# Unread products, an earlier first block and other ties in a planned instruction order of a four-layer sequence kernel

## The chip, the cores and the metric

The kernel runs on one core of a Trainium2 chip. A core has five engines with a queue each, run in order: TensorE (PE, matrix products; PEld is its weight load), VectorE (DVE), ScalarE (ACT), GpSimd (POOL) and SyncE (SP, which here only issues transfers). The time is device microseconds of one launch. The runs of the kernel before took 2665.15 us in the median of three (2664.05 to 2667.85).

## The reference, cut to what matters

The input is a batch of 32 elements of 256x256 numbers in float32. Each element passes through four layers one after the other; no element depends on another.

```python
def reference(x, ...):                      # x: (32, 256, 256)
    # layer 0: block norm over the whole 256x256, scale and shift made from a time step
    out = silu(scale * layer_norm(x) + shift) @ W_in + b_in
    x = silu(scale * layer_norm(out) + shift) @ W_out + b_out + x
    # layer 1: attention with 16 heads of 16, a bias of 16x256x256 per element and a mask, FF 1024
    x = ln(x) * (1 + scale1) + shift1
    scores = q @ k / 4 + attention_bias     # masked to -inf
    x = x + softmax(scores) @ v @ Wo + bo
    x = x + gelu_sigmoid((ln(x) * g2 + beta2) @ W1 + b1) @ W2 + b2
    # layer 2: finite differences of x times fixed grids, one step in time, max(., 0)
    x = maximum(x + df * dt, 0)
    # layer 3: causal attention with 16 heads, FF 1024, a gate between its input and output
    return x + gate * (block(x) - x)
```

Scale and shift of layers 0 and 1 come from two small networks on sine and cosine encodings of one number per element. They are made once for all 32 elements, ahead of the first element.

## The kernel before, in words

**Tiles.** An element is a tile of 128 partitions x 2 x 256. A full product has a 128x128 stationary operand and streams 256 columns into a PSUM bank; a transpose is a product with the identity that streams 128. In float32 each plain product stands in the trace as two records, a transpose as one. Two kinds of product use small tiles of PE's array: the scores (`scores`, line 834; 32 rows by 128 columns, groups of 8 products that run side by side) and the weighted values (`values`, line 885; 128 rows by 32 columns, groups of 16). All eight PSUM banks are one pool with the tag `bank`; a PSUM tile is named `mm`, `sc` (scores) or `tr` (transposed probabilities).

**Layers.** `layer_0` (line 990), `layer_1` (1015) and `layers_23` (1071) are generators, one per element. `layer_0` makes `offset` on POOL from `beta_t` and the shift, the block statistics in `block_stats` (759; two products with one column each against `mean_mat`), and in `scaled_silu` (780) the row scale `rs` on POOL, `y` on DVE, a Tanh on ACT and a last step on DVE, whose result `th` goes into the products with `l0_win` and, after a second pass, `l0_wout`. `layer_1` reads 16 heads of bias through the tile `nb` (three buffers), subtracts the mask on POOL, adds the bias to the scores on DVE, takes the exponential on ACT (`pr`), transposes it on PE (`turned`, 868) and multiplies by the values. `layers_23` computes the finite differences with the products against `stencil`, then the causal attention and the feed-forward whose hidden tile `hid` is put through Gelu in one ACT instruction (`gelu_all`).

**Setup** (lines 542 to 650): encodings on DVE with Sin on ACT; `conditioning` (606) is a group of small products with `l0w1`, `l0w2`, `l0wss` or `w_ada` streamed, a copy to `by_batch`, a transpose and an add. The three calls in a row for layer 0 make `mod0`, then halved; the fourth makes `mod1`. `gamma_t` and `beta_t` are transposed copies of the tiles `l0gb`. `load_x` (536) loads an element; the first one is loaded ahead of the layers. `turned_vectors` (521) brings in bias vectors as rows (`as_rows`), by 14 small transfers for the second block of them, and transposes them into `cols`. The other weights are loaded by `load_attention`, `load_rest` and `loads`; `load_rest` has a product of `wo` with a bias vector (`L1wo<-cols` and `L3wo<-cols` in the profile), so that PE waits for these two weights to land.

**What sets the order.** No engine call goes out when it is written. `Order` (line 65) records each one with a length, its dependencies and a rank, the time `order.now` at which it is due. `trace` (1155) sets the rank: a layer of element b starts at `b * PERIOD + START[i] + EDGE[b, i]`, each `yield` moves it on by its step times `PACE[i]`, and `SHIFT` corrects single steps. `arrange` (217) then plans: it plays the five engines forward and, whenever one is free, lets it take the ready unit of the lowest rank. A unit is one instruction or, under `together`, a group of products. Its constants stand for the hardware: `HOPS` is the time from an instruction's end to a dependent one on another engine, to which `SLACK` is added when the dependent one is on PE, `CAPS` limits the PSUM tiles of each name, `EARLIER` makes PE's ranks earlier by name, `STAY` and `FRESH` add to a unit's rank on PE if it changes the shape of the array:

```python
                    if e == "pe" and units[u][2][0]["length"][1] != shape:
                        rank += self.STAY
                        if units[u][2][0]["length"][1] != (P, P):
                            rank -= self.PAIR if shape != (P, P) else 0.0
                        elif units[u][2][0]["length"][3] == 2:
                            rank += self.FRESH
```

So `FRESH` falls on a full product (two records) that would follow a small-tile group, and not on a transpose. `emit` (377) issues all calls in the planned order; every instruction stands on the line 382 in the profile (383 after the change). An engine then runs its instructions strictly in that order and waits where an operand or a bank is not ready.

Of the kernel before, what the change touches and what calls it, by code (L numbers as in the profile page):

```python
# [16 lines left out]
AF = mybir.ActivationFunctionType  # L17
# [4 lines left out]
P = 128  # L22
# [16 lines left out]

PERIOD = 86.0
START = (-61.8, 0.0, 116.9)
PACE = (1.55, 1.23, 1.08)
EDGE = {(0, 0): 14.4, (0, 1): -5.0, (0, 2): 5.8, (1, 0): -19.0, (1, 1): -3.8, (1, 2): -0.2, (2, 0): -27.1, (2, 1): -2.0, (2, 2): -1.1, (3, 0): 12.3, (3, 1): 0.4, (3, 2): 0.3, (4, 0): 5.2, (4, 1): 2.3, (4, 2): 0.6, (27, 0): -1.1, (27, 1): -1.0, (27, 2): 0.5, (28, 0): 1.7, (28, 1): -0.3, (28, 2): -2.0, (29, 0): 2.1, (29, 1): -0.1, (29, 2): -2.1, (30, 0): -11.1, (30, 1): 5.7, (30, 2): -4.5, (31, 0): -16.9, (31, 1): 1.9, (31, 2): 15.4}
SHIFT = (
    {0: -93.0, 1: -33.6, 2: -27.5, 3: -32.8, 4: -14.7, 5: -56.4, 6: -42.3, 7: -28.3, 8: 23.1},
    {0: -9.7, 1: -80.2, 2: -10.3, 3: -1.7, 4: 2.7, 5: 8.8, 7: -7.0, 8: 14.7, 9: -90.2, 11: 7.3,
     12: 21.2, 13: -0.4, 14: 4.0, 15: -1.3, 16: 11.4, 17: 5.1, 19: 4.8, 20: 10.4, 21: 46.1, 22: 16.4,
     23: -8.7, 24: -13.1, 25: -30.4, 26: -2.4, 27: -90.0, 28: 8.3, 29: -134.0, 30: -0.4, 31: -13.2,  # L50
     32: -34.6, 33: 0.8, 34: -0.3, 35: 7.7, 36: -2.9, 37: -8.0},
    {0: -1.1, 1: -32.9, 2: -9.3, 3: 27.2, 4: 23.9, 5: -25.6, 6: -48.6, 7: -36.4, 8: -12.9, 9: 6.6,
     11: 3.0, 12: 15.4, 13: -32.5, 15: -6.5, 16: 20.0, 17: -2.0, 18: 6.6, 19: -0.5, 20: 0.4, 21: -82.2,
     23: 9.0, 24: 7.5, 25: 0.1, 26: -11.0, 27: -38.3, 28: 12.2, 29: 7.0, 30: 30.4, 31: 3.6, 32: -8.7,
     33: -46.1, 34: 4.4, 35: 2.3, 36: -58.5, 37: -16.3, 38: -59.7, 39: 18.0, 40: -15.2, 41: 12.6},
    {0: -24.5, 1: -13.3, 2: 6.7, 3: -84.2, 4: 42.8},
)
NORM = 8.0
LAND = 3.0
SQUARE = 2.0  # L60
# [4 lines left out]
class Order:  # L65
# [11 lines left out]
    TURN = 92.0  # L77
    FIRST = {(32, P): 107.0, (P, 32): 27.0, (P, P): 107.0}
    APART = 120.0
    SLACK = 50.0  # L80
    SEEN = {(32, P): 165.0, (P, 32): -16.0, (P, P): 165.0}
    CAPS = {"sc": 8, "tr": 7, "mm": 7}
    EARLIER = {"sc": 29.6, "mm": -2.0, "tr": 6.2}
    STAY = 5.0
    FRESH = 1.0
    PAIR = 0.0
    PORT = 0.05
    TABLES = {AF.Sin: 0, AF.Tanh: 1, AF.Exp: 1, AF.Gelu: 2}
# [342 lines left out]
def kernel(ctx: ExitStack, tc: tile.TileContext, io, out, n_batch=B):  # L431
    nc = tc.nc
    order = Order()
    pe, dve, act, pool, sync = (
        order.engine(name, eng)
        for name, eng in (
            ("pe", nc.tensor), ("dve", nc.vector), ("act", nc.scalar), ("pool", nc.gpsimd), ("sync", nc.sync)
        )
    )
# [8 lines left out]
    ident = ctile("ident", [P, P])  # L448
# [28 lines left out]
    mod0 = ctile("mod0", [P, 2 * C2, B])  # L477
# [19 lines left out]
    def mm_tile(shape):  # L497
        return psum_tile(shape, "mm")
# [37 lines left out]
    def load_x(b):  # L536
        x = sb.tile([P, C2, D], F32, tag="x", name="x")
        sync.dma_start(x, rows(io["x"][b]))
        return x
# [9 lines left out]
    )  # L549
    w1 = sb.tile([P, 4 * E], F32, tag="t2", name="l0w1", bufs=3)  # L550
    sync.dma_start(w1, io["L0_cond_W1"])
    i_b = sb.tile([P, B], I32, tag="nq1", name="i_b")
    sync.dma_start(i_b, io["itok_B_34_63"].partition_broadcast(P))
    w2 = sb.tile([P, 4, 4 * E], F32, tag="hid", name="l0w2", bufs=1)
# [1 line left out]
    wss = sb.tile([P, 2, 4, D], F32, tag="pt", name="l0wss", bufs=3)  # L556
    sync.dma_start(wss[:, 0], rows(io["L0_cond_Wsc"]))
    sync.dma_start(wss[:, 1], rows(io["L0_cond_Wsh"]))
    first_x = load_x(0)
    gb = []  # L560
    for n in ("gamma", "beta"):
        t = sb.tile([P, C2, D], F32, tag="l2", name="l0gb", bufs=4)
# [16 lines left out]
    def cosine(dst, a, r, parts=slice(0, P)):  # L579

        dve.tensor_scalar(a, r, -1.0, None, ALU.mult)
        dve.tensor_tensor(a, a, r, ALU.max)
        dve.tensor_scalar(a, a, -1.0, math.pi / 2, ALU.mult, ALU.add)
        act.activation(dst[parts], a[parts], AF.Sin)

    small = sb.tile([P, 16, B], F32, tag="pr", name="encodings", bufs=10)
    x0, r0, n0, a0, enc, x1f, r1, n1, a1, emb0, emb1 = (small[:, i] for i in range(11))
# [8 lines left out]
    reduced(r1, n1, x1f)  # L596
    act.activation(emb0, r1, AF.Sin)
    cosine(emb1, a1, r1)

    def silu(dst, zh, th, z):  # L600

        dve.tensor_scalar(zh, z, 0.5, None, ALU.mult)
        act.activation(th, zh, AF.Tanh)
        dve.scalar_tensor_tensor(dst, th, 1.0, zh, ALU.add, ALU.mult)

    def conditioning(dst, weights, src, bias):


        pm = mm_tile([P, P])
        with order.together():  # L610
            for k in range(len(weights(0))):
                for j in range(4):
                    pe.matmul(
                        pm[j * B : (j + 1) * B, :], lhsT=src[:, k, :], rhs=weights(j)[k],
                        start=k == 0, stop=k == len(weights(0)) - 1,
                    )
        by_batch = sb.tile([P, P], F32, tag="h_t", name="by_batch")
        dve.tensor_copy(by_batch, pm)
        pm = mm_tile([P, 4, B])
        pe.transpose(pm.rearrange("p j b -> p (j b)"), by_batch, ident)  # L620
        dve.tensor_tensor(dst, pm, bias.unsqueeze(2).broadcast_to([P, 4, B]), ALU.add)
# [6 lines left out]
    part = lambda j: slice(j * P, (j + 1) * P)  # L628
    conditioning(h1, lambda j: [w1[:, part(j)]], enc.unsqueeze(1), vector["L0_cond_b1"])
    silu(h1s, zh, th, h1)  # L630
    conditioning(h2, lambda j: [w2[:, k, part(j)] for k in range(4)], h1s, vector["L0_cond_b2"])
    both = cols0[:, 8:12]
    conditioning(mod0, lambda j: [wss[:, j // 2, k, part(j % 2)] for k in range(4)], h2, both)
# [7 lines left out]
    for i, e in enumerate((emb0, emb1)):  # L641
# [9 lines left out]
    sync.dma_start(parity, io["c_parity"])  # L651
    order.now = START[0] + 5.0
    _, more = turned_vectors(
        "cols1",
        (
            "L1_cond_bq", "L1_cond_bk", "L1_cond_bv", "L1_cond_b1", "L1_cond_g2", "L1_cond_beta2",
            "L3_cond_bq", "L3_cond_bk", "L3_cond_bv", "L3_cond_b1", "L3_cond_gamma1", "L3_cond_beta1", "L3_cond_gamma2", "L3_cond_beta2",
        ), sync,
    )
# [3 lines left out]
    def col(name):  # L663
        return vector[name]
# [33 lines left out]
    def loads():  # L698

        load_rest(l1, "L1", "g2", "beta2")  # L700
        yield LAND

        edge = sb.tile([P, 3, 2, 4], F32, tag="pr", name="edge", bufs=10)
        sync.dma_start(edge, io["c_edge"].rearrange("p (k e x) -> p k e x", k=3, e=2))
        a1 = sb.tile([P, C2, D], F32, tag="l2", name="a1", bufs=4)
        sync.dma_start(g_a0, rows(io["L2_cond_A_grid"][0]))
        sync.dma_start(a1, rows(io["L2_cond_A_grid"][1]))
        sync.dma_start(g_b0, rows(io["L2_cond_B_grid"][0]))
        sync.dma_start(g_b1, rows(io["L2_cond_B_grid"][1]))
        sync.dma_start(g_b2, rows(io["L2_cond_B_grid"][2]))  # L710
        later.stencil = ctile("stencil", [P, 2, C2, NEAR])
        sync.dma_start(later.stencil, io["c_stencil"])
        later.dt_b = load_row("dt_b", io["condB_dt"])
        yield 3 * LAND
        dve.tensor_scalar(g_b0, g_b0, 0.5, None, ALU.mult)
        dve.tensor_scalar(g_b2, g_b2, 0.5, None, ALU.mult)
        dve.tensor_tensor(g_cp, g_b1, a1, ALU.subtract)
        dve.tensor_scalar(g_cp, g_cp, 0.5, None, ALU.mult)
        dve.tensor_tensor(g_cm, g_b1, a1, ALU.add)
        dve.tensor_scalar(g_cm, g_cm, 0.5, None, ALU.mult)  # L720
        e_t = sb.tile([P, C2, 2, 4], F32, tag="small", name="small")
        for c in range(C2):
            dve.tensor_tensor(e_g[:, c], edges4(g_b2)[:, c], edge[:, 0], ALU.mult)
            dve.tensor_tensor(e_t[:, c], edges4(a1)[:, c], edge[:, 1], ALU.mult)
            dve.tensor_tensor(e_dd[:, c], edges4(g_b1)[:, c], edge[:, 2], ALU.mult)
        dve.tensor_tensor(e_dd, e_dd, e_t, ALU.add)
        yield 3 * LAND
        later.l3 = load_attention("L3")
        sync.dma_start(causal, io["c_causal"])
        later.l3_g1, later.l3_beta1 = col("L3_cond_gamma1"), col("L3_cond_beta1")  # L730
        yield 3 * LAND
        load_rest(later.l3, "L3", "gamma2", "beta2")
        later.gate_b = load_row("gate_b", io["condB_gatescore"])
# [421 lines left out]
    def trace(n, gen, layer, start, pace):  # L1155
        i = 0
        while True:
            order.now = start + SHIFT[layer].get(i, 0.0)
            step = next(gen, None)
            if step is None:  # L1160
                break
            start += step * pace
            i += 1

    trace(3 * n_batch, loads(), 3, START[1] + 25.0, 1.0)
    res = {}
    for b in range(n_batch):
        for i, layer in enumerate((layer_0, layer_1, layers_23)):
            trace(3 * b + i, layer(b, res), i, b * PERIOD + START[i] + EDGE.get((b, i), 0.0), PACE[i])
    with tc.manual_schedule():  # L1170
        order.emit()
# [33 lines left out]
```

## Time and profile before

| what | value |
|---|---|
| median of three runs | 2665.15 us |
| the profiled execution | 2665.54 us |
| its span, first to last instruction | 2663.7 us |
| PE, DVE, ACT, POOL busy | 2600.2, 2122.1, 1920.1, 1565.0 us |
| mean granted clock of PE | 0.989 |
| PE's first product starts | 5.52 us |
| last product of the run ends, store follows | 2658.2 us |
| longest waits of PE up to 132 us | 5.5 (first rows of vectors), 3.3 and 3.4 (`th`), 2.8 (encodings), 2.6 (`t`), 2.5 (`x`) |
| longest waits of PE from 2585 us | 4.2 and 3.7 (`hid`), 3.7 (`t`) |

Busy time is the union of an engine's records, so waits and idle time are the rest. The granted clock is what the throttle let PE have: 1.00 or 0.50 at each moment, averaged over a stretch. The timeline merges equal instructions in a row: start, length from the first start to the last end, engine, line, operation, tiles, shape, count, and in brackets the idle time before and what ended it. Ends of products are modelled; starts are not, so prices below are taken from start to start. In the tables of stretches the columns are the stretch, its length, the busy time (and number of records) of PE, PEld, DVE, ACT and POOL, the granted clock, the DMA engines' share and GB/s.

### The profile page before, as it was taken

What the parts mean: (1) busy time and instruction counts of PE and PEld (TensorE: products, weight loads), DVE (VectorE), ACT (ScalarE), POOL (GpSimd) and SP (SyncE); (2) the same over time, 40 slices, a digit from 0 to 9 for tenths busy, and PEclk for the clock granted to TensorE, in tenths of its full rate; (3) what the DMA queues carried; (4) which work ended last, traced back from release to release, by engine and by line L of the source; (5) the groups of instructions that cost most, each with busy time, mean ns of one, the idle gap of its engine ahead of it and who ended that gap; (6) DMA issues with size and microseconds to landing.
All of it is one profiled execution on the core that took longest, in us unless ns stands there. A gap on an engine that the chain in (4) does not pass through costs nothing.

```text
span 2663.7 us, 60400 instructions
## 1 busy us (share of the span) xinstructions
PE 2600.2 (98%) x20462; PEld 2118.4 (80%) x20462; DVE 2122.1 (80%) x7627; ACT 1920.1 (72%) x6120; POOL 1565.0 (59%) x1960
## 2 busy tenths in 40 slices
PE   5999999999999999999999999999999999999997
PEld 4777888888888888888888888888888888888775
DVE  5887888878878877878878878877878887887853
ACT  2677777877777877777777777877777877777854
POOL 3865676555676555576555677555576555676420
PEclk7999999999999999999999999999999999999998
DMA  7321122212122212122212122212122211122100
GB/s 243 110 60 59 42 73 69 70 49 66 45 70 70 70 49 66 46 70 69 70 49 65 43 73 70 69 49 66 46 69 69 70 57 57 42 69 64 45 5 9
DMA packets 177064, 169.69 MB, mean 64 GB/s; under 512 B 19514, under 2 KB 175220, under 8 KB 176756
## 3 DMA queue, kind: packets, MB, share of 16 engines
q1 hardware_dynamic: 176720, 165.82, 20.2%
q8 instruction: 163, 2.67, 0.4%
q14 instruction: 145, 1.19, 0.1%
q10 hardware_dynamic: 36, 0.01, 0.0%
HBM read 157.40 MB, written 8.39 MB: 62 GB/s over the span
## 4 chain that ended last, share of the span: by engine, by line
PE 91%; DVE 3%; ACT 2%; DMA 1%; POOL 1%; issue 1%; SPq 0%; ACTq 0%; POOLq 0%; DVEq 0%
PE mm L382 68%; PE tr L382 14%; PE sc L382 9%; DVE pr L382 1%; ACT hid L382 1%; ACT pr L382 1%; DMA x<-in_x_dram 1%; POOL nb L382 0%; DMA nb<-in_fside_Bx16xSxS_dram 0%; DVE pt L382 0%; ACT L382 0%; POOL rstd L382 0%; DVE gd L382 0%; DMA L1wo<-in_L_cond_Wo_dram 0%; DVE st L382 0%
## 5 line engine op out<-in xcount | busy, mean ns | idle before, releaser
L382 ACT ACTIVATE pr<-pr,mn 128x256 f32<-128x256 f32 (+1 forms) x2048 | 966.9, 478 | 93.0 <-DVE mn L382 91.8
L382 POOL TENSOR_TENSOR nb<-mask_f,nb 128x512 f32<-128x512 f32 x512 | 693.3, 1378 | 114.7 <-DMA nb<-in_fside_Bx16xSxS_dram 101.9
L382 PE MATMUL tr<-ident,pr 128*128 128x128 f32 x3584 | 508.5, 276 | 5.4 <-ACT pr L382 1.8
L382 PEld LDWEIGHTS tr<-ident,pr 128*128 128x128 f32 x3584 | 419.5, 143 | 85.8 <-ACT pr L382 29.1
L382 DVE CUSTOM_DVE_ANT_0 pr<-sc,nb 128x256 f32<-128x256 f32 x1024 | 388.0, 414 | 25.3 <-POOL nb L382 14.0
L382 ACT ACTIVATION_READ_ACCUMULATOR pr<-pr,mn 128x1 f32 x2048 | 398.0, 194 | 0.0
L382 DVE COPY pt<-tr 128x512 f32<-128x512 f32 (+1 forms) x512 | 311.3, 615 | 72.9 <-PE tr L382 72.3
L382 POOL TENSOR_SCALAR hid<-hid 128x256 f32<-128x256 f32 x256 | 100.0, 405 | 433.4 <-ACT hid L382 433.1
L382 DVE CUSTOM_DVE_ANT_0 pr<-sc,causal 128x128 f32<-128x128 f32 (+1 forms) x1024 | 299.3, 352 | 38.5 <-PE sc L382 37.2
L382 PE MATMUL sc<-k_t,nq 32*128 32x256 f32 (+1 forms) x4096 | 269.5, 375 | 0.1
L382 ACT COPY pt<-tr 128x512 f32<-128x512 f32 (+1 forms) x512 | 261.4, 526 | 10.9 <-PE tr L382 6.0
L382 PE MATMUL mm<-L3w,hid 128*128 128x256 f32 x1024 | 241.5, 385 | 10.1 <-ACT hid L382 10.0
L382 PE MATMUL mm<-h_t,L3w 128*128 128x256 f32 x1024 | 247.6, 382 | 1.5 <-DVE h_t L382 1.4
L382 PE MATMUL mm<-h_t,L1w 128*128 128x256 f32 x1024 | 248.9, 381 | 0.0
L382 PE MATMUL mm<-L1w,hid 128*128 128x256 f32 x1024 | 239.0, 380 | 0.1
L382 PEld LDWEIGHTS sc<-k_t,nq 32*128 32x128 f32 x4096 | 163.3, 185 | 73.0 <-issue 25.7
L382 PEld LDWEIGHTS mm<-L3w,hid 128*128 128x128 f32 x1024 | 190.6, 193 | 35.1 <-ACT hid L382 11.9
L382 POOL COPY wide<-rs 128x256 f32<-128x256 f32 x128 | 53.3, 416 | 281.3 <-DVE rs L382 131.8
L382 PEld LDWEIGHTS mm<-L1w,hid 128*128 128x128 f32 x1024 | 186.6, 190 | 23.3 <-issue 1.2
L382 PEld LDWEIGHTS mm<-h_t,L3w 128*128 128x128 f32 x1024 | 184.2, 191 | 22.9 <-DVE h_t L382 2.5
L382 PEld LDWEIGHTS mm<-h_t,L1w 128*128 128x128 f32 x1024 | 183.7, 190 | 23.3 <-issue 1.8
L382 ACT ACTIVATE t<-x,shift,rstd 128x256 f32<-128x256 f32 x128 | 67.2, 590 | 148.8 <-DVE shift L382 148.8
(173 smaller groups left out, 4997.7 us busy)
## 6 DMA issues: line engine op xcount, KB each, us to landing
nb<-in_fside_Bx16xSxS_dram SPq DMA_DIRECT2D x512, 256.0 KB
x<-in_x_dram SPq DMA_DIRECT2D x32, 256.0 KB
out_dram<-d SPq DMA_DIRECT2D x32, 256.0 KB
mask<-in_mask_Bx1xSxS_bk_dram SPq DMA_DIRECT2D x32, 64.0 KB
L1w<-in_L_cond_W_dram SPq DMA_DIRECT2D x2, 1024.0 KB
L3w<-in_L_cond_W_dram SPq DMA_DIRECT2D x2, 1024.0 KB
l0w<-in_L_cond_W_dram SPq DMA_DIRECT2D x1, 1024.0 KB
g_b<-in_L_cond_B_grid_dram SPq DMA_DIRECT2D x3, 256.0 KB
```

Source lines behind the costliest of these rows:

```text
L382: call(*args, **kwargs)
```

## The change

There are four parts.

1. The constants of the planner: `PERIOD`, `START`, `PACE`, `EDGE`, `SHIFT`, and in `Order` `SLACK` from 50 to 0, `CAPS` of `sc` from 8 to 7 and of `tr` from 7 to 5, `EARLIER`, and `FRESH` from 1 to 16.
2. The first element's `x` is loaded right behind `l0w1`, layer 0 of that element is due far earlier (`EDGE[0, 0]` is -796), and what follows the first `silu` of the setup is due at -960 instead of -1000.
3. An ACT instruction of one column with Tanh behind the last cosine.
4. `fill` records products of 64 columns that nobody reads, with a rank so late (1e6) that PE takes one in the plan only where nothing else is ready: 150 that read `mod0`, and 100 that read the last element's output of layer 1.

```diff
-PERIOD = 86.0
-START = (-61.8, 0.0, 116.9)
-PACE = (1.55, 1.23, 1.08)
-EDGE = {(0, 0): 14.4, (0, 1): -5.0, (0, 2): 5.8, (1, 0): -19.0, ...}
+PERIOD = 85.9
+START = (-61.2, 0.0, 116.1)
+PACE = (1.45, 1.23, 1.08)
+EDGE = {(0, 0): -796.0, (0, 1): -5.1, (0, 2): -0.1, (1, 0): -50.0, ...}
...
+FILL = (150, 100)
...
-    SLACK = 50.0
+    SLACK = 0.0
-    CAPS = {"sc": 8, "tr": 7, "mm": 7}
-    EARLIER = {"sc": 29.6, "mm": -2.0, "tr": 6.2}
+    CAPS = {"sc": 7, "tr": 5, "mm": 7}
+    EARLIER = {"sc": 26.8, "mm": -3.3, "tr": 5.8}
-    FRESH = 1.0
+    FRESH = 16.0
...
     sync.dma_start(w1, io["L0_cond_W1"])
+    first_x = load_x(0)
...
-    first_x = load_x(0)
...
     cosine(emb1, a1, r1)
+    act.activation(a1[:, 0:1], emb1[:, 0:1], AF.Tanh)
...
     silu(h1s, zh, th, h1)
+    order.now = -960.0
...
+    def fill(count, src):
+
+        order.now = 1e6
+        for _ in range(count):
+            pe.matmul(mm_tile([P, P // 2]), lhsT=src, rhs=ident[:, 0 : P // 2], start=True, stop=True)
+
+    fill(FILL[0], mod0.rearrange("p j b -> p (j b)"))
     trace(3 * n_batch, loads(), 3, START[1] + 25.0, 1.0)
...
         for i, layer in enumerate((layer_0, layer_1, layers_23)):
+            if (b, i) == (n_batch - 1, 2):
+                fill(FILL[1], res[1, b][:, 0, 0:P])
```

`SHIFT` changes in nearly all its entries, by a few us in most and by up to 110 in single ones.

## Prediction

> **What bounds the kernel now.** I read the page first, then busy time by stretches, then TensorE's own sequence in the first 60 and the last 80 us.
>
> ```profile
> span 2663.7 us, 60400 instructions
> PE 2600.2 (98%) x20462; PEld 2118.4 (80%) x20462; DVE 2122.1 (80%) x7627; ACT 1920.1 (72%) x6120; POOL 1565.0 (59%) x1960
> PEclk7999999999999999999999999999999999999998
> PE 91%; DVE 3%; ACT 2%; DMA 1%; POOL 1%; issue 1%; SPq 0%; ACTq 0%; POOLq 0%; DVEq 0%
> ```
>
> TensorE (PE) is the bound and carries 91% of the chain that ended last. By stretches (columns: length, then PE, PEld, DVE, ACT, POOL busy, granted clock, DMA):
>
> ```profile
> 23.90:132.10 108.20, 88.16 (x573) 66.93 (x573) 78.02 (x263) 56.22 (x176) 71.00 (x87) 0.84 0.55 171
> 300.00:2400.00 2100.00, 2097.78 (x16695) 1720.12 (x16694) 1727.27 (x6207) 1573.06 (x5017) 1283.79 (x1603) 1.00 0.20 61
> 2585.80:2663.70 77.90, 57.53 (x317) 42.15 (x316) 27.45 (x107) 33.01 (x97) 6.66 (x11) 0.85 0.02 7
> ```
>
> In the middle PE waits 2 us in 2100: there only PE's own work counts. At both ends it waits, and runs at a reduced clock (0.84 and 0.85). I priced PE's whole sequence by the median start-to-start of each pair of neighbours in the middle: 2548.7 us of work at full clock, of which 4.5 lie before 24 us, 76.2 before the first stencil product (132.1 us) and 40.8 behind 2585.8. The other 115.0 us of the span are waits and half clock: 56.0 before 132.1, 6.8 from there to 300, 10.1 in the middle, 5.0 from 2400, 37.1 at the end (5.5 of it the last DVE steps and the store).
>
> **Part 1, ties behind small tiles (FRESH 1 to 16, SLACK 50 to 0, CAPS, the retuned times).** All 12606 old products stay, in another order. PE's timeline gives the price of a change of shape:
>
> ```profile
> 2541.46 0.94 PE L382 MATMUL sc<-k_t,nq 32*128 32x128 f32 x16
> 2542.32 1.13 PE L382 MATMUL mm<-L3wv,h_t 128*128 128x256 f32 x4
> 2543.29 0.60 PE L382 MATMUL mm<-ident,t 128*128 128x128 f32 x4
> 2543.73 1.89 PE L382 MATMUL mm<-L3w,hid 128*128 128x256 f32 x8
> ...
> 1004.76 1.03 PE L382 MATMUL mm<-h_t,L3w 128*128 128x256 f32 x4
> 1005.62 0.60 PE L382 MATMUL tr<-ident,pr 128*128 128x128 f32 x4
> ```
>
> Four records of a full product take 1005.62-1004.76 = 0.86 us, but 2543.29-2542.32 = 0.97 behind a small-tile group (scores, values): 0.10 more. A transpose is 0.109 (0.44 for four), the first behind a small group 0.056 more. The turn itself costs 0.093 (309 ns start to start where 216 is usual). In the two instruction orders a regular element has 22 turns before and 21 after, full products straight behind small groups 3 and 1, transposes there 7 and 8: 0.093 + 2x0.104 - 0.056 = 0.25 us less. Pair by pair over the whole order: 79.50 to 79.23 per element, 2548.7 to 2542.4 in all, **-6.3**. DVE, ACT and POOL keep their instructions and wait on nothing new. A regular element shows 0.2 us of waits now (79.71 between stencils); I leave it, because the distance in PE work between what feeds a transpose, product or score and its use is much the same in both orders (shortest 2.4 us for transposes before, 1.8 after; median 8.6 in both). From below: nothing gained, if other waits come; above: the 0.2 too, 5 us.
>
> **Part 2, first x ahead, its statistics, an early Tanh.** x (256 KB) goes from SP's eighth transfer to its fourth, so w2, the two wss and i_b land about 0.75 us later (256 KB took 0.75 here), and everything behind keeps its byte count. The statistics are done by some 9 us instead of 23.4. It buys nothing: the first W_in product needs y, y needs rs, and POOL makes rs behind offset, which needs mod0 halved; the new DVE order puts that halving behind the copy of the second vector block, whose rows end PE's wait at 22.87. So POOL offset 23.5 to 24.6 (1.09), rs 0.26, y 0.88, tanh 0.63, last step 0.69: 27.3, as now (27.25). Both l0gb transposes now stand ahead of the second conditioning and need beta, landed about 14.4; at half clock (0.23 each) it starts near 15.4 instead of 14.83, hidden by the wait to 22.87; uncovered it would be 0.6. The dummy Tanh and the Sin now split in two cost two more table loads, 2x1.28 us on ACT, inside its 7.2 us of idle before 18.9; uncovered, 2.6. Sum: 0.
>
> **Part 3, the 250 unread products.** Each is two records of 64 columns with 128 columns of weights, on banks last used some seven products earlier. Price: the nearest rows are the transpose, also 128 columns of weights, 0.109 a record, so 0.218; and the one-column statistics products, 0.030 + 0.112 = 0.142 behind long ones. The Trainium skill ("TensorE: Matmul & The Clock Gate", section LDWEIGHTS) says that a weight load takes as long as its columns, 128/1.2 = 107 ns whatever the streamed length: an estimate of 0.214. I take 0.218: 250 are 54.5 us (35.5 at the low end), queued ahead of real work on an in-order engine. They pay only as far as they stand where PE idles and hold its clock. What holds it is shown by stretches of 3.41 us between the clock's changes:
>
> ```profile
> 21.62:25.04 3.42, 1.14 (x8) 0.88 (x8) 1.05 (x6) 0.00 (x0) 1.86 (x5) 1.00 0.70 221
> 28.45:31.86 3.41, 2.59 (x7) 1.50 (x5) 0.00 (x0) 0.79 (x2) 1.23 (x2) 0.50 1.15 299
> 42.10:45.52 3.42, 2.70 (x7) 1.61 (x5) 1.18 (x4) 0.00 (x0) 0.00 (x0) 0.50 0.98 303
> 45.52:48.93 3.41, 1.10 (x4) 0.68 (x4) 3.15 (x12) 0.00 (x0) 1.41 (x3) 1.00 0.81 236
> 66.00:69.41 3.41, 2.05 (x14) 1.49 (x14) 2.18 (x6) 2.31 (x9) 1.39 (x2) 1.00 0.73 232
> 69.41:72.82 3.41, 1.56 (x12) 1.30 (x12) 3.03 (x13) 2.65 (x9) 3.41 (x3) 1.00 0.10 7
> ```
>
> Counting streamed columns (128 per 0.107 us at full clock), stretches of 0.25 and less lose the clock (21.62, 45.52, 69.41), one of 0.35 keeps it (66.00) while 0.37 and 0.43 late in the run lose it, and it comes back after 0.73 (42.10) but not after 0.70 (28.45). An unread product streams 0.107 of 0.218, 0.49: **enough to hold a full clock, not to win it back alone**. The skill's rule (same page, Part 1) of an idle window that halves the clock would say that the products hold it everywhere; the rows say a stretch with 1 us of wait left falls to 0.35 and loses it. By the page the sum below is 4 us lower; I go by the rows.
>
> *Head.* From 23.9 us (the last by_batch transpose, as now) to the first stencil the new order has 75.4-4.2 = 71.2 us of work and 131 unread products, 28.6. Still ended by DMA are L1wo (32.7; 18+7 products and W_in end at 31.1: 1.6 left) and L3wo (46.5; 0.5 left); 1.5 more in the first attention. The stretch to 25.04 holds about 0.33, so I count one loss of clock there: 13 products at 0.45 and W_in cold, caught up partly at L1wo, 3.2 net. Stencil at 23.9+71.2+28.6+3.6+3.2 = 130.5, 1.6 ahead of 132.1, with 0.8 less work behind it: -0.8. Up to 300 us the last 19 (4.1) and 0.8 replace 6.8: -1.9. **Head -2.7.**
>
> *Tail.* Until 2585.8: 5 products (1.1) and 3.2 for 5.0: -0.7. Behind it 95, 20.7 us, for 37.1: with 5.5 at the end, 1.3 of the last wait (hidden layer: identity, table load 1.28, gelu 1.91, 4.15 in all, 13 products fill 2.8), 1.7 elsewhere (the 21 behind L3wo take 4.6 where the wait was 3.7, so 0.9 too many) and 1.0 for a clock lost in two: 30.2, **-6.9**.
>
> Sum against the profile's own span: 2663.7 - 6.3 - 2.7 - 0.7 - 6.9 = 2647.1. The profiled execution took 2665.54 in all, the median of the runs 2665.15, 1.45 over the span: **2648.5 us**.
>
> **Rivals.** (a) *All clocks held, shorter products*: 4 us of cold and 2 of surplus go, 2642. For: 0.49 is above every stretch that lost the clock; against: single waits remain. (b) *The regular element picks up waits* since the planner no longer allows 50 ns before PE: each 0.1 us costs 2.6 over 26 elements; 0.3 gives 2656, 0.6 eats the gain. For: 50 ns is taken from every hop to PE; against: of 1426 first uses between 600 and 2200 us only 9 start within 150 ns of their producer's end. (c) *Slower: unread products that stay cold.* Place: the 72 before the first layer_1's transposes. If the clock drops at 25.04 and pure 0.49 cannot lift it, each costs 0.47 for 0.218 and stands ahead of W_in, W_out and the transposes. 72x0.25 = 18, less the 3.2 counted, and 7 of real products at half clock: 2670. It decides from 66 cold ones (16.6/0.25). For: the rise at 0.73 only; against: W_in, L1wo and W_out between them make fuller stretches. (d) *Unread products only replace waits and the order gives nothing*: 2662.
>
> **How the numbers follow.** Likeliest 0.64 (its own range 2641 to 2656), (a) 0.12, (b) 0.12, a quarter of it within 0.2%, (c) 0.08, (d) 0.04. 0.2%, about what a measurement of this kernel can tell from no change, is 5.3 us: faster 0.64+0.12+0.09 = 0.85, same 0.07, slower 0.08. The range 2637 to 2667 leaves out half of (a)'s low side and (c).
>
> **What would show it.** Stencil to stencil 79.4 in the middle (80 or more: b). Clock rows of 1.0 from 30 us to the end, with a dip at 25 (long halves: c). Unread products at 0.22 us a pair in a row. First W_in product at 27 to 31 us and L3wo still ended by DMA at 46.5. From the last stencil to the end 75 instead of 82. I am wrong if L1wo and L3wo land elsewhere or if the products' bank waits show as PE idle.

## The result, and the profile after

The changed kernel takes 2688.17 us (median of four runs, 2682.21 to 2693.15) against 2665.11 for the kernel before on the same chip: 1.0085 times the time, 95% interval 1.0073 to 1.0096. The forecast was 2648.5, so the change costs 23 us where it was to gain 17.

The page of the changed kernel, profiled in an execution of 2691.58 us: its span and instruction count, the busy times, the granted clock in 40 slices, the chain that ended last.

```profile
span 2689.8 us, 61313 instructions
PE 2652.3 (99%) x20962; PEld 2173.5 (81%) x20962; DVE 2143.9 (80%) x7627; ACT 1937.3 (72%) x6123; POOL 1554.8 (58%) x1960
PEclk9999999999999999999999999999999999999999
PE 90%; ACT 4%; DVE 3%; DMA 1%; POOL 1%; issue 1%; SPq 0%; ACTq 0%; DVEq 0%; POOLq 0%
```

By this page all is as the forecast wanted it: PE is busy for 99% of the span, and the clock has no weak slice left (the profile counts it as full up to its first recorded change, at 34.09 us here; what the products ahead of that show stands under the head). Only the chain has moved: ACT's share went from 2% to 4%, 1% of PE's is gone. Busy time by stretches (columns: stretch, length, then PE, PEld, DVE, ACT, POOL busy, granted clock, DMA share, GB/s) tells more.

```profile
300.00:2400.00 2100.00, 2086.90 (x16533) 1702.88 (x16532) 1727.52 (x6137) 1568.66 (x4965) 1261.15 (x1585) 1.00 0.20 61
2614.16:2689.80 75.64, 69.33 (x539) 60.75 (x537) 28.71 (x109) 35.90 (x104) 8.86 (x13) 0.98 0.02 8
```

In the middle PE's busy time fell by 11 us (2097.78 before), and it put 162 fewer records through in the same 2100 us: it waits. The last stretch, from the last element's stencil to the end, is as forecast, 75.6 us for 82.0, at a clock of 0.98 for 0.85.

I read the distances between the first stencil products of consecutive elements out of PE's timeline, where one begins as in these two lines (the timeline's columns are start, length, engine, line, operation, tiles, shape, count):

```profile
1259.52 0.39 PE L383 MATMUL mm<-stencil,gd 128*128 128x129 f32 x2
...
1340.09 0.39 PE L383 MATMUL mm<-stencil,gd 128*128 128x129 f32 x2
```

A regular element takes 80.57 us, where the kernel before took 79.71 and the forecast had 79.4. The whole difference of the spans, 2689.8 - 2663.7 = 26.1 us, splits into +7.0 up to the first stencil product (139.10 instead of 132.14), +25.5 between the first and the last, and -6.4 behind the last. The +7.0 belongs to this one execution: e1_pe_order and e3_both_orders below, with the same order on every engine up to there, have 133.04 and 132.40.

**Where the middle waits.** Pricing each pair of neighbours on PE as in the forecast, a regular element of the changed kernel has 79.23 us of work, so it waits 1.34 us; it had waited 0.21. Of this, 1.21 us lie at one place, behind the second group of scores in layer 3's attention: pair by pair against e2_act_order below, which has the same sequence on PE, nothing else in the element differs by more than 0.03. ACT and PE there, in the timeline of the changed kernel (in brackets the idle time before, and what ended it):

```profile
1286.48 0.94 PE L383 MATMUL sc<-k_t,nq 32*128 32x128 f32 x16
1286.73 0.63 ACT L383 ACTIVATE th<-y 128x512 f32<-128x512 f32 x1 [0.16 <-DVE y L383]
1287.35 1.13 PE L383 MATMUL mm<-L3wv,h_t 128*128 128x256 f32 x4
1288.52 0.37 ACT L383 COPY L3v<-mm 128x256 f32<-128x256 f32 x1 [1.17 <-PE mm L383]
1288.91 1.28 ACT L383 ACT_TABLE_LOAD   x1
1290.14 0.94 PE L383 MATMUL sc<-k_t,nq 32*128 32x128 f32 x16
1290.21 0.40 ACT L383 ACTIVATE pr<-pr,mn 128x128 f32<-128x128 f32 x1
1291.01 0.33 PE L383 MATMUL tr<-ident,pr 128*128 128x128 f32 x1
1291.51 0.71 PE L383 MATMUL tr<-ident,pr 128*128 128x128 f32 x3 [0.18 <-ACT pr L383]
1292.39 0.44 PE L383 MATMUL tr<-ident,pr 128*128 128x128 f32 x2 [0.16 <-ACT pr L383]
1292.66 0.60 PE L383 MATMUL mm<-ident,t 128*128 128x128 f32 x4
```

Six transposes that need 6 x 0.109 = 0.65 us take from 1291.01 to 1292.66, in small pieces that wait for ACT's `pr`. The first exponential began only at 1290.21, though its scores had been there since 1287.4 and DVE's first minimum since 1287.7: on ACT it stands behind the copy of `L3v`, which waited 1.17 us for a product of PE, and behind the table load. The same place in the kernel before:

```profile
1268.29 0.94 PE L382 MATMUL sc<-k_t,nq 32*128 32x128 f32 x16
1268.39 1.28 ACT L382 ACT_TABLE_LOAD   x1
1269.16 1.13 PE L382 MATMUL mm<-L3wv,h_t 128*128 128x256 f32 x4
1269.69 0.40 ACT L382 ACTIVATE pr<-pr,mn 128x128 f32<-128x128 f32 x1
1270.58 0.34 ACT L382 COPY L3v<-mm 128x256 f32<-128x256 f32 x1
1271.09 0.66 PE L382 MATMUL mm<-ident,t 128*128 128x128 f32 x4
1271.58 0.49 PE L382 MATMUL tr<-ident,pr 128*128 128x128 f32 x3
```

There the load runs while PE makes the scores, the exponential follows 0.5 us behind them, and the copies come between exponentials. Two moves matter here: on ACT the copy went ahead of load and exponential, on PE the four transposes of `t2` went behind the six.

**The head.** PE's own sequence from the last `by_batch` transpose, for the changed kernel (the unread products are the ones of shape 128x64):

```profile
24.55 7.78 PE L383 MATMUL mm<-ident,mod 128*128 128x64 f32 x36
32.12 2.92 PE L383 MATMUL mm<-th,l_win 128*128 128x256 f32 x8
40.58 8.48 PE L383 MATMUL mm<-ident,mod 128*128 128x64 f32 x40
48.85 3.09 PE L383 MATMUL mm<-l_wout,th 128*128 128x256 f32 x8
```

36 records in 7.78 us are 0.216 a record and 40 in 8.48 are 0.212, twice the 0.109 of the forecast: the products run at half clock, the first row because in this execution the clock did not rise before 34.09 at all, the second because it fell again at 40.92. `l_win` starts at 32.12 instead of 27.25, `l_wout` at 48.85 instead of 41.05. Further on, at full clock, a record takes 0.107 to 0.114 from row to row (0.112 inside a row), about the 0.218 a product that was priced.

### The profile page after: what moved, and what is told of

It is laid out like the page before. It is cut to its first block, busy times and chain, and to the rows that moved or that the text cites. A ratio compares the mean times of both kernels' runs of the same rounds, so it can differ in the third digit from the quotient of the medians.

```text
span 2689.8 us, 61313 instructions
## 1 busy us (share of the span) xinstructions
PE 2652.3 (99%) x20962; PEld 2173.5 (81%) x20962; DVE 2143.9 (80%) x7627; ACT 1937.3 (72%) x6123; POOL 1554.8 (58%) x1960
## 3 DMA queue, kind: packets, MB, share of 16 engines
q14 instruction: 143, 1.17, 0.2%
## 4 chain that ended last, share of the span: by engine, by line
PE 90%; ACT 4%; DVE 3%; DMA 1%; POOL 1%; issue 1%; SPq 0%; ACTq 0%; DVEq 0%; POOLq 0%
PE mm L383 68%; PE tr L383 14%; PE sc L383 8%; ACT pr L383 2%; ACT L383 1%; DVE pr L383 1%; DMA nb<-in_fside_Bx16xSxS_dram 1%; ACT L3v L383 1%; DVE pt L383 1%; POOL nb L383 0%; DVE gd L383 0%; DMA l0gb<-in_L_cond_gamma_dram 0%; ACT hid L383 0%; SPq L383 0%; DVE b2f L383 0%
## 5 line engine op out<-in xcount | busy, mean ns | idle before, releaser
L383 POOL TENSOR_TENSOR nb<-mask_f,nb 128x512 f32<-128x512 f32 x512 | 686.0, 1364 | 42.1 <-DMA nb<-in_fside_Bx16xSxS_dram 37.5
L383 PE MATMUL tr<-ident,pr 128*128 128x128 f32 x3584 | 525.2, 278 | 8.8 <-ACT pr L383 8.4
L383 POOL COPY wide<-rs 128x256 f32<-128x256 f32 x128 | 61.3, 479 | 362.1 <-DVE rs L383 335.6
L383 DVE DVE_READ_ACCUMULATOR2_ANT mn<- 128x1 f32 x2048 | 167.9, 82 | 0.0
```

The lines of the kernel that those rows point to most:

```text
L383: call(*args, **kwargs)
```

## The experiments

Unless said otherwise an edit is made on the changed kernel. Medians of the kernel before on the same chips were 2665.5 to 2666.6. "Regular" is the median distance from stencil to stencil of elements 9 to 24; first stencil and tail (last stencil to end) are of the one profiled execution.

| kernel | median us | ratio to before, 95% | regular | first stencil | tail |
|---|---|---|---|---|---|
| before | 2665.11 | 1 | 79.71 | 132.14 | 82.0 |
| after | 2688.17 | 1.0085 (1.0073 to 1.0096) | 80.57 | 139.10 | 75.6 |
| e1_pe_order | 2686.28 | 1.0078 (1.0063 to 1.0093) | 80.57 | 133.04 | 75.7 |
| e2_act_order | 2654.89 | 0.9958 (0.9943 to 0.9973) | 79.36 | 137.11 | 74.0 |
| e3_both_orders | 2662.63 | 0.9987 (0.9976 to 0.9998) | 79.62 | 132.40 | 75.7 |
| e4_wide_fill | 2682.16 | 1.0057 (1.0040 to 1.0074) | 80.58 | 131.06 | 74.6 |
| f1_act_wide | 2653.58 | 0.9956 (0.9943 to 0.9968) | 79.36 | 130.32 | 74.6 |
| f2_act_no_fill | 2666.26 | 1.0000 (0.9992 to 1.0009) | 79.51 | 130.19 | 78.8 |
| f3_before_first_x_tail | 2665.02 | 0.9997 (0.9989 to 1.0006) | 79.71 | 135.34 | 79.1 |
| f4_slack_50 | 2697.00 (one) | one execution | 80.60 | 141.81 | 77.9 |
| g1_before_copy_first | 2714.55 | 1.0186 (1.0172 to 1.0200) | 81.63 | 132.98 | 82.2 |
| g2_before_first_x | 2668.19 | 1.0010 (1.0004 to 1.0017) | 79.71 | 133.24 | 80.2 |
| g3_act_tail_only | 2658.69 | 0.9974 (0.9963 to 0.9984) | 79.68 | 132.53 | 74.6 |
| h1_early_table | 2654.30 | 0.9957 (0.9940 to 0.9973) | 79.36 | 130.86 | 74.6 |

**e1_pe_order: PE's order at the place.**

```diff
...
+        pe = sorted((u for u in self.units if u[0] == "pe"), key=lambda u: u[2][0]["start"])
...
+        for a, b, c in zip(pe, pe[1:], pe[2:]):
+            if has(a, "tr") and has(b, "tr") and len(a[2]) == len(b[2]) == 3 and has(c, "t2"):
+                for i, x in enumerate(c[2]):
+                    x["start"] = a[2][0]["start"] - 1.0 + 0.1 * i
```

> The changed kernel with one move on TensorE alone: in layer 3's first attention pass of every element, the block of four t2 transposes stands ahead of the six probability transposes that follow the second scores group, as it did in the kernel before; ACT, DVE, POOL and SP keep their order. Theory A (the new due times put these transposes right behind the scores, where ACT's exponentials are not there yet; in the changed kernel's trace they wait about 1.1 us per element at this one place): the block covers 0.6 of it; stencil to stencil 79.9 to 80.0 instead of 80.57, total about 2688 - 26 x 0.6 = 2672. Theory B (the missing 50 ns of slack lets every hop to TensorE come late, so that the wait moves to the next place): 80.4 or more, total within 4 us of 2688.

Measured: 80.57, unchanged, so this form of theory A was wrong. PE at the place in this kernel:

```profile
1284.87 0.66 PE L392 MATMUL mm<-ident,t 128*128 128x128 f32 x4
1285.37 0.72 PE L392 MATMUL tr<-ident,pr 128*128 128x128 f32 x4
1286.25 0.71 PE L392 MATMUL tr<-ident,pr 128*128 128x128 f32 x3 [0.16 <-ACT pr L392]
1287.12 0.44 PE L392 MATMUL tr<-ident,pr 128*128 128x128 f32 x2 [0.17 <-ACT pr L392]
```

The block of `t2` fills the first wait, and the later transposes wait longer for it: they are paced by the exponentials, one about every 0.44 us. When ACT's row of exponentials sets the end, work put ahead of the first transposes only moves the waits back. The regular element being equal, the 1.9 us between the two medians are not put down to this edit.

**e2_act_order: ACT's order at the place.**

```diff
...
+        act = sorted((u[2][0] for u in self.units if u[0] == "act"), key=lambda x: x["start"])
...
+        for a, b in zip(act, act[1:]):
+            if out(a).startswith("L3v") and out(b).startswith("pr"):
+                a["start"] = b["start"] + 1.0
```

> The changed kernel with one move on ACT alone: the copy of L3v goes behind the first exponential of that attention pass, so that the table load of the exponential no longer queues behind a copy that waits for TensorE's value product; TensorE's order is the changed kernel's. Theory A (ACT is late at this one place because copy and table load stand in this order): table load about 1.1 us earlier, waits at the place from 1.1 to about 0.3 us per element, stencil to stencil 79.7 to 79.9, total about 2668. Theory B (slack, spread over all hops): no change, 80.57 and 2688.

Measured: 79.36 and 2654.89. The edit moves both copies of `L3v` one place back, so that the first exponential leads; in an element's order on ACT that is all that changes. It takes 1.21 us off every regular element and 33.3 us off the median, more than expected. ACT and PE in its timeline:

```profile
1272.20 1.28 ACT L391 ACT_TABLE_LOAD   x1
1273.50 0.40 ACT L391 ACTIVATE pr<-pr,mn 128x128 f32<-128x128 f32 x1
1273.90 0.35 ACT L391 COPY L3v<-mm 128x256 f32<-128x256 f32 x1
1275.84 0.88 PE L391 MATMUL tr<-ident,pr 128*128 128x128 f32 x6
```

The load starts 0.9 us behind the start of the first scores (1271.31) instead of 2.4 us (1286.48 to 1288.91), and the six transposes go through in one piece. With 79.36 the element is 0.13 above its priced work. (The 26 regular elements give 31.5 of the 33.3; the rest is within the spread of the changed kernel's four executions.)

**e3_both_orders: both moves.**

> Both moves together. Theory A: the place waits no more, stencil to stencil 79.4 to 79.5 (79.23 of priced work and the 0.2 of the kernel before), total about 2688 - 26 x 1.1 = 2659. Theory B: 80.4 or more, 2684 to 2688.

Measured: 79.62 and 2662.63 (2656.33 to 2669.74), slower than e2 alone and a little above what was expected. PE no longer waits at the transposes; instead the `h_t,L1wq` products behind them start 158 and 104 ns late, once per element each: 0.26, the difference from 79.36. So PE's new order at this place was the better one, given exponentials in time.

**g1_before_copy_first: the mirror, on the kernel before.**

```diff
...
+        for a, b, c in zip(act, act[1:], act[2:]):
+            if out(c).startswith("L3v") and out(a).startswith("pr") and out(b).startswith("pr"):
+                c["start"] = max(a["start"] - 1.0, made[c["call"][1][1].tensor.name] + 0.5)
+                a["start"] = max(a["start"], c["start"] + 0.1)
+                b["start"] = max(b["start"], c["start"] + 0.2)
```

> The mirror of e2_act_order on the kernel before: in every element ACT's copy of L3v is put ahead of the first exponential of layer 3's first attention pass, and with it ahead of the table load; nothing else moves, and TensorE keeps the old order. If ACT's order alone is the cause: the copy has to wait for TensorE's value product (it ends near 1270.2 in the profile of before, where the table load began at 1268.39), so the first exponential comes about 2.2 us later and the first three transposes, 1271.58 in that profile, 1.4 us later; stencil to stencil 79.71 + 1.4 to 1.9, so 81.1 to 81.6, total 2666 + 26 x 1.4 to 1.9 = 2702 to 2715. If TensorE's order were needed for the wait as well: 79.7 to 80.0, 2666 to 2672.

Measured: 81.63 and 2714.55, at the top of what was expected. The copy waits for the value product, and the load with it:

```profile
1294.23 0.37 ACT L397 COPY L3v<-mm 128x256 f32<-128x256 f32 x1 [1.95 <-PE mm L397]
1294.62 1.28 ACT L397 ACT_TABLE_LOAD   x1
1295.92 0.40 ACT L397 ACTIVATE pr<-pr,mn 128x128 f32<-128x128 f32 x1
1296.46 0.33 PE L397 MATMUL tr<-ident,pr 128*128 128x128 f32 x1 [0.81 <-ACT pr L397]
```

The order of one copy against load and exponential makes the wait in either kernel, with PE's order untouched in both.

**f4_slack_50: SLACK.**

```diff
-    SLACK = 0.0
+    SLACK = 50.0
```

> The changed kernel with SLACK back at 50. The instructions of a regular element stand in the same order on TensorE, DVE, ACT and POOL as with SLACK 0, so that theory A (the due times made the order) expects 80.57 us between stencils, unchanged, and 2684 to 2692 in all; theory B (SLACK made the waits): 79.7 to 80.0 and about 2668.

Measured: 80.60, one execution of 2697.00, 5 us above what was expected; its first stencil came latest of all, at 141.81. `SLACK` does not make the waits of the regular element. With the old `CAPS`, too, the planned order of a regular element is the same on all four engines; with `FRESH` at 1 one pair of products on PE, one instruction on DVE and one on ACT stand elsewhere. That leaves the due times. With `START` alone put back, both its changed entries together, the plan has the copy behind the exponential again, as in the kernel before; with `PERIOD`, the last table of `SHIFT` or one of the two entries alone it stays ahead. The other due times, put back alone, give no complete plan. These are plans; none of them was run.

**h1_early_table: the load ahead of the Tanh, nothing moved.** Both in the kernel before and after, ACT loads tables twice an element: ahead of Gelu and ahead of the first exponential. In the planner's table (line 89) Tanh belongs to the exponential's set: after Gelu it puts 1.3 us on layer 0's Tanh, `th<-y` at 1286.73 above, and none on the exponential. In the timeline that Tanh runs without a load, and the exponential pays. The Trainium skill ("ScalarE: Activation LUTs", Table sets: the hidden batching unit) names tanh with the exponential's set and not with Gelu's, as the planner does; the trace decides, and it has the load behind the copy. To test it, a one-column exponential goes ahead of the Tanh on e4_wide_fill (the changed kernel with wider unread products, below):

```diff
             call, args, kwargs = x["call"]
+            if len(args) > 2 and args[2] == AF.Tanh and args[0].tensor.name.startswith("th0"):
+                call(args[0][:, 0, 0:1], args[1][:, 0, 0:1], AF.Exp)
             call(*args, **kwargs)
```

> e4_wide_fill with one small instruction more: ahead of each of layer 0's two Tanh, ACT takes the exponential of one column, which the Tanh then writes over. Nothing moves: the copy of L3v still stands ahead of the first exponential of layer 3's attention, but the table load of the exponential now comes ahead of the Tanh, where the planner counts it, instead of behind the copy. Theory A' (the planner puts the load before the Tanh and takes the exponentials to be 1.3 us earlier than they are, so that the load behind the copy is what is late): first exponential about 1.1 us earlier, waits of the transposes behind it from 1.2 to 0.1 to 0.3 us, stencil to stencil 79.4 to 79.7, total 2682 - 26 x 1.0 = about 2656. Rival (the copy's wait for TensorE's value product is what is late, and the load goes with it): 80.3 to 80.6 and 2677 to 2683.

Measured: 79.36 and 2654.30, 27.9 us less than e4_wide_fill. ACT and PE at the place:

```profile
1266.23 1.28 ACT L384 ACT_TABLE_LOAD   x1
1267.00 1.13 PE L385 MATMUL mm<-L3wv,h_t 128*128 128x256 f32 x4
1267.53 0.20 ACT L384 ACTIVATE th<-y 128x1 f32<-128x1 f32 x1
1267.76 0.63 ACT L385 ACTIVATE th<-y 128x512 f32<-128x512 f32 x1
1268.30 0.35 ACT L385 COPY L3v<-mm 128x256 f32<-128x256 f32 x1
1268.55 0.40 ACT L385 ACTIVATE pr<-pr,mn 128x128 f32<-128x128 f32 x1
1270.66 0.87 PE L385 MATMUL tr<-ident,pr 128*128 128x128 f32 x6
```

The copy stands where the change put it and does no harm. The load and the Tanh now fill the time in which the copy would wait for PE's value product, and the exponential follows at once. What was late was the load in line behind that wait; taking either out of the other's way, as here or in e2, is enough. In the kernel before the misjudged load cost next to nothing: it fell right behind `k_t`, beside PE's scores and DVE's first minimum, which ends at 1269.54, 0.15 us before the exponential begins.

**e4_wide_fill: products of 128 columns.**

```diff
-            pe.matmul(mm_tile([P, P // 2]), lhsT=src, rhs=ident[:, 0 : P // 2], start=True, stop=True)
+            pe.matmul(mm_tile([P, P]), lhsT=src, rhs=ident, start=True, stop=True)
```

> The changed kernel with unread products of 128 columns instead of 64, same count, same order; a record stays 0.109 at full clock, but then streams nearly all of it. Theory A (what brings the clock back is the share of streamed columns; a 64-column product has 0.49 and cannot): in the head the half clock lasts at most 7 us in all instead of the 10 and more us from 40.9 to 51.2 and the stretch up to 34.1, first stencil at about 131 instead of 139, total about 2680, regular element unchanged at 80.57. Rival: the clock is brought back by work of real products only, or the products' own time is the cost: first stencil within 1.5 us of 139, total 2688.

Measured: first stencil 131.06, 2682.16, 6.0 us less in the medians, though the four executions of each overlap (2681.99 to 2684.85, and 2682.21 to 2693.15 with narrow products). What is clear is the trace: twice the columns cost nothing, because a record takes 0.112 inside a row with either, and the clock, once up at 18.05 us, stays up for the whole head.

**f1_act_wide: e2 and e4 together.**

> The changed kernel with ACT's copy of L3v behind the first exponential (as in e2_act_order) and unread products of 128 columns (as in e4_wide_fill). If the two causes are independent: regular element 79.36, first stencil 131 instead of 137.1, tail 74 to 75, total 2654.9 less some 6 = 2649. If the gain of the head was given back before the middle in e4_wide_fill: 2654 to 2655.

Measured: 2653.58, 0.9956 of the kernel before, the best of all here with h1_early_table (2654.30). It is not the 2649 expected of independent causes. Beside e2_act_order the wide products are worth 1.3 us, about what the kernel before differs by between chips, and not the 6.8 by which the first stencils of the two profiles differ: e2's profiled execution was its longest, 2658.63 us. PE's head in this kernel, to be held against the changed kernel's above:

```profile
23.59 5.87 PE L391 MATMUL mm<-ident,mod 128*128 128x128 f32 x36
29.30 1.89 PE L391 MATMUL mm<-th,l_win 128*128 128x256 f32 x8
37.03 4.71 PE L391 MATMUL mm<-ident,mod 128*128 128x128 f32 x40
41.58 1.89 PE L391 MATMUL mm<-l_wout,th 128*128 128x256 f32 x8
```

The clock drops here too, at 24.38, but comes back at 27.80. What each width does within one whole stretch of the clock is in these rows. The first three are the changed kernel's: narrow products with one-column statistics products between them, then narrow ones alone, twice.

```profile
37.50:40.92 3.42, 3.42 (x33) 3.42 (x32) 2.66 (x10) 0.00 (x0) 1.56 (x4) 1.00 1.10 348
40.92:44.33 3.41, 3.41 (x18) 3.41 (x18) 1.56 (x3) 0.63 (x1) 3.12 (x7) 0.50 1.11 351
44.33:47.75 3.42, 3.42 (x18) 3.42 (x18) 1.65 (x4) 0.00 (x0) 0.37 (x1) 0.50 1.04 289
```

The next is e3_both_orders', nearly all narrow products, and the last f1_act_wide's, wide products alone:

```profile
40.99:44.40 3.41, 3.41 (x31) 3.41 (x31) 2.40 (x5) 0.63 (x1) 2.69 (x5) 1.00 1.10 339
24.38:27.80 3.42, 3.42 (x18) 3.42 (x18) 1.57 (x3) 0.63 (x1) 0.55 (x2) 0.50 0.91 277
```

PE is busy throughout in all five. Two stretches of narrow products in a row leave the clock at half; one of wide products brings it back. A full clock stays full behind e3's stretch of narrow products, and is lost at 40.92 behind the one that has the statistics between them: 23 x 64 columns, 0.36 of the stretch when counted as in the forecast.

**f2_act_no_fill and g3_act_tail_only: what the unread products are worth.** f2 is e2_act_order with `FILL = (0, 0)`, g3 is f1_act_wide with `FILL = (0, 100)`.

> e2_act_order without any unread product. Theory A (in the head the narrow products cost as much as the half clock that they were to hold off; in the tail they hold it): first stencil 131 to 133 (137.1 and 139.1 with them), tail 81 to 82 instead of 74 to 75.6, total 2654.9 - 4 + 7 = 2658. Rival (the products gain the 2.7 us of the forecast in the head, and the new order alone is slower there): first stencil 139 or later, total 2664 or more. Rival (the clock at the end rises by itself in the new order): tail 75 to 76, total 2651.

> f1_act_wide with the 100 unread products of the tail alone, none in the head. If the head's products are worth nothing once their columns are wide (first stencil 130.3 with them, 130.2 in the profile without any): 2652 to 2656, tail 74 to 75, first stencil 130 to 132. If they steady the clock in the head and behind it (f2_act_no_fill lay between 2659.5 and 2670.9): median 2657 to 2662, with a drop of the clock near 80 us and a first stencil of up to 135 in the slower executions.

Measured: 2666.26 (2659.51 to 2670.94) without any, 8 above the 2658 expected; 2658.69 (2655.55 to 2661.32) with those of the tail, as the second case of g3 expected; 2653.58 with both. In the medians the products of the tail are worth 7.6 us and those of the head 5.1, each with what comes with them: without them the planner also puts some real work near the place in another order. The single profiles don't give the shares. f2 and g3 have no products in the head and the same order there, and their first stencils stand at 130.19 and 132.53 (f2's profile is of its shortest execution), with 130.32 in f1. The tail is 74.6 with products and 78.8 without. In g3's profile the clock drops at 70.5 and at 84.2, where f1's stays up from 27.80 on; but 2.9 of the 5.1 us between these two profiles lie behind the first stencil, at full clock, where more of g3's elements are about 1 us long. Why is open.

**f3_before_first_x_tail and g2_before_first_x: part 2.** g2 is the kernel before with part 2 alone; f3 adds 100 wide products ahead of the last pass.

> The kernel before with only part 2 (first x ahead, its statistics, the early Tanh, the -960) and 100 unread products of 128 columns ahead of the last element's last pass; its planner constants, due times and EDGE are the old ones, and its regular element has the old order. Part 2 forecast at nothing: first W_in product at about 27.3 and first stencil at 132 (131.5 to 133); tail 75 to 76 instead of 82, total 2666 - 6.5 = 2659. If the early statistics bring the first stencil forward: 2657 or less; if w2 and wss behind x make it late: 2661 or more. Regular element 79.71.

> The kernel before with part 2 alone (first x ahead, its statistics, the early Tanh, the -960), no unread products, old constants. The forecast has it at nothing: 2666, first stencil 131.5 to 133. If part 2 costs what f3_before_first_x_tail showed (first stencil 135.3, 3.2 late): 2669. If that lateness was another placing of the clock's drops: between 2664 and 2668 with the first stencil anywhere between 130 and 136, and single executions some us apart.

Measured: g2 2668.19, 2.0 us slower than the kernel before beside it. Its first W_in product starts at 26.83, `L1wo` at 32.59 and `L3wo` at 46.00, so the transfers and POOL's chain came as the forecast said; but the clock is at half from 26.12 to 56.84 in one piece, where the kernel before had it at full from 45.5 to 48.9 and again from 55.75. From 25 us to the first stencil that makes 37.6 us at half clock instead of 34.1, and the first stencil 1.1 us later. f3 missed its 2659: 2665.02, with a tail of 79.1 instead of 75. In the old order of the tail the products bring 1.1 to 2.9 us (80.2 in g2, 82.0 before), not 6. Why the old order profits less was not tested.

## Why the prediction was wrong, point by point

**Part 1: the price was right, "a regular element shows 0.2 us of waits now; I leave it" was the step that failed.** The working behind it counted PE work between what feeds a transpose and its use. At the place that failed this distance even grew: from the scores to the first transposes PE has 3.3 us before (1268.29 to 1271.58) and 4.5 after (1286.48 to 1291.01). A distance in PE work does not see what else stands in line: the lateness arose on ACT's own queue, where the copy waits for PE and the table load stands behind it, and it costs 1.21 us an element where the step had nothing. That queue was not walked through; "DVE, ACT and POOL keep their instructions and wait on nothing new" is true of the instructions and false of the waits. With the exponentials in time, e2_act_order, f1_act_wide and h1_early_table show 79.36, where the forecast had 79.4, 0.13 above the priced 79.23: the 0.27 us from turns and ties agree with that, though no run took them out alone.

**Rival (b)** had the place and the sign (waits in the regular element) and the wrong cause. It named the 50 ns of `SLACK`; f4_slack_50 shows 80.60 with them back. Its price, 2.6 us per 0.1 us, fits: 1.21 us would be 31.5, and the medians of the changed kernel and e2 are 33.3 apart.

**Part 2: nothing forecast, 2.0 us lost,** a tenth of a percent. The times of the steps were right. The clock, which was not counted there, was at half for 3.4 us more in g2's profile; that this is the whole of the 2.0 is not shown.

**Part 3, head: -2.7 forecast, +7.0 in the profiled execution, +0.9 and +0.3 in those of e1 and e3.** The reading that the narrow product can hold the clock but not win it back was right (e3's stretch from 40.99, the changed kernel's from 40.92). One of the readings behind it was not: of the stretches late in the run of before, the one at 0.43 (2629.40 to 2632.82, 7 records) kept its full clock, and of two at 0.38 (from 2622.58 and 2656.71) the first lost it, so the border lies lower and is not sharp. The step that failed here is the size of the loss. The sum counted one loss with 13 cold products and had the clock caught up near `L1wo`; the trace has about 73 cold records, some 37 products, in two rows alone, the first because the clock had not risen before them, and half clock again until 51.16. In e1 and e3 the clock is lost at 24.69 and 23.92, where the forecast had it, and is back only 10.2 us later. That is rival (c)'s mechanism at its place, with fewer cold products than its 66; one cost 0.21 more, where (c) had 0.25. With wide products the first stencil comes at 130.3 to 131.1, where the forecast had 130.5 for its one loss; f2, without any product there, has 130.19, so that this is no proof of a gain. `L3wo` was not ended by DMA but stood behind late work, at 55.55. For the page's rule on idle windows ("TensorE: Matmul & The Clock Gate", Part 1), which would have had the products hold the clock everywhere, these rows speak as those of before did: from 37.50 to 40.92 PE was busy for 3.42 of 3.42 us and lost the clock, and from 40.92 to 47.75 it was busy throughout and did not get it back.

**Part 3, tail: right in the number, by luck in part.** 75.6 us from the last stencil to the end where 75 was forecast, and the clock at 0.98. The forecast gave the whole gain to the products. But with no products at all, and an order that differs a little there, the profile of f2 has 78.8, so that about half of the 6.4 comes with the new order, and in the old order the products bring only 1.1 to 2.9.

**The sum.** From the forecast's 2648.5 to the measured 2688.2 there are 39.7 us: 33.3 are the late exponentials (e2), 1.3 the narrow products (f1 against e2; 6.0 beside the waits, e4; neither clear of the spread), and 5.1 remain in f1. In its profile they lie between first and last stencil: seven of its elements take 0.3 to 1.3 us more than 79.36, with stencil products that wait 0.92 for DVE's `gd` three times and hidden products of layer 1 that wait 0.5 to 1.2 three times. Their cause is open.

## What to carry to other kernels

On a kernel whose bound engine is full, a new order has to be judged on the other engines' queues too: follow each engine that feeds it through its instructions in order, and ask of every table load what it stands behind. A planner's model of such a load is worth checking against one line of the trace; here a load that the planner put at the wrong instruction was free in one order and cost 1.2 us per element in the next. Where unread products are to bring a clock back, try the wider ones first: here those of 128 columns did it, those of 64 did not, and both took 0.112 us a record.

## What the runs showed that I had not expected

- A Tanh behind Gelu needed no table load (1286.73 in the changed kernel), and the exponential behind the load began 1.30 us after the load's start (1288.91 to 1290.21): the load cost its 1.28 us and next to nothing more.
- At half clock a record of 64 columns takes as long as one of 128, 0.21 us, and PE is shown busy in both. Only the wide ones raised the clock, within one stretch of 3.42 us.
- The moment at which the clock first rises differs between executions with the same order in the head: 17.1, 17.9, 22.6 and 34.1 us in four profiles with narrow products (e3, e1, e2, after). In those the first stencil came at 132.4, 133.0, 137.1 and 139.1, so that one profile of such a head says little about its median.
